# A mixture-of-experts layer: where the shared expert's last product stands between wide and single expert jobs

## The chip, the core and the metric

The kernel runs on one core of a Trainium2 chip. The metric is device time in microseconds (us) of one whole execution; three executions of the kernel before gave 2105.7, 2106.51 and 2108.94 us, with a median of 2106.51 us. PE is the matrix engine, DVE the vector engine, ACT the scalar engine, POOL the general-purpose engine, and SP the engine that here only issues transfers. All of them run their own instruction streams and meet through semaphores.

## The reference, cut to what matters

Two graph layers run over 625 nodes of 1024 features. Each adds a graph branch, an attention branch and a feed-forward branch. The change lies in the last piece, the feed-forward branch of the second layer: a small attention, a router that sends every node to two of eight experts, and a shared expert that sees every node.

```python
logits = xf @ Wr.T + expert_bias
rw = jax.nn.softmax(logits, axis=-1)
topw, topi = jax.lax.top_k(rw, TOP_K)          # TOP_K = 2 of 8 experts
topw = jax.nn.softmax(topw, axis=-1)
...
shared = _swiglu(xf, sW1, sW2, sW3)             # silu(x @ W1.T) * (x @ W3.T) @ W2.T
...
eo = jnp.einsum('etf,edf->etd', h, eW2)         # the same form for every expert
specialist = jnp.einsum('te,etd->td', combine, eo)
moe_out = (shared + specialist).reshape(B, S, d)
return X + moe_out
```

The shared expert's last product is the multiplication by `sW2`, a matrix of 1024 by 1024 in float32 (4 MB).

## The kernel before, in words

Nodes stand in NT = 5 tiles of P = 125 rows. Everything is float32, and a product of two float32 tiles shows in the profile as two matrix instructions.

**What comes before.** The shared expert's first two products make `hT`, all nodes' hidden values turned so that the features lie on the partitions. They are made by `eighth(0)` and `eighth(1)`, each with seven smaller products (a Strassen scheme, named p1 to p7 by their role). The second of them runs p1, p2, p6, p7, p4, p5, p3. The products p1, p2 and p4 read the tile `tT` (the normalised nodes, turned); p5, p6, p7 and p3 read sums made from it. p4 is the last to read `tT`. Up to this point the order of every engine, SP too, is the order in which the program is written (`hand`, a manual schedule, closed on L2192). After it the Tile scheduler orders instructions inside each basic block, unless another manual schedule is opened.

**The routed experts.** The router's counts are made on the chip. Each expert's nodes are cut into blocks of up to 128 rows, and two jobs exist for them. A wide job (`wide_job`, L2242) takes up to 192 rows of an expert at once, with the weights as the stationary operand. A single job (`block`, L2214) takes one block of 128 rows. Each job loads three 4 MB matrices of its expert in twelve transfers of 1 MB on SP (`Half`, L126, six buffers of tag `w` for the first two matrices and four of tag `mid` for the third), fetches its rows with an indirect transfer on POOL (`take`, L2201), turns them on PE (`turned`, L2211), multiplies, and writes its result to the DRAM table `y_d`.

**Branches.** How many jobs there are is known only on the chip. So `wides` (L2284), `odd` (L2290) and `fours` (L2296) are nested `If`s; every engine loads the count into a register (`count_of`, L2280) and branches for itself. An engine that leaves the branch without taking it first waits for its own earlier work and then raises its semaphores by what the skipped jobs would have raised, so that later waits still count right. On this input the profile shows two wide jobs, no odd block and eight blocks in two groups of four.

**The shared expert's last product.** After the wide jobs, SP is told to load `sW2` in eight transfers of 512 KB: `k` 0 to 4 into a buffer of tag `big`, 5 to 7 into the buffer of tag `CT` (L2308). `big` has two buffers; at that time one holds `hT`, and the other `three`, the single tile with the wide jobs' three operands (rows turned, hidden values, result). `sw2` takes the buffer of `three`.

**The end.** After the last block, PE, DVE and POOL follow a hand-written order. `fetch(t)` (L2325) gathers a node tile's two expert results from `y_d` with two indirect transfers into buffers of tags `xg` and `yb` (two of each); `shared(t)` (L2331) multiplies one node tile by `sW2`, in two groups of eight products into one PSUM bank each (`ps1`, two buffers), and DVE adds each half to `x` (L2336); `routed(t)` (L2340) adds the two gathered results on DVE; SP writes the tile out (L223). The order is `fetch(0)`, `fetch(1)`, then for each tile but the last `shared`, `routed`, `fetch(t + 2)`, and for the last one `routed` before `shared`.

Of the kernel before, what the change touches and what calls it, by code (L numbers as in the profile page):

```python
# [8 lines left out]
FP = mybir.dt.float32  # L9
# [5 lines left out]
ALU = mybir.AluOpType  # L15
# [6 lines left out]
P = 125  # L22
NP = 626
# [6 lines left out]
D = 1024  # L30
KC = D // 128
NE = 8
# [3 lines left out]
WIDE = 192  # L36
# [19 lines left out]
def attempt(ctx: ExitStack, tc: tile.TileContext, w: dict, out: bass.AP, shifted: bool):  # L56

    nc = tc.nc
# [6 lines left out]
    def ps1(name):  # L65
        pool, n = psums[-1]
        return pool.tile([128, 512], FP, tag="ps1", name=name, bufs=n)

    def ps2(name):
        return psums[-1][0].tile([128, 2, 512], FP, tag="ps2", name=name, bufs=3)  # L70
# [65 lines left out]
    def group(dst, pairs):  # L136

        for i, (lhsT, rhs) in enumerate(pairs):
            made = nc.tensor.matmul(dst, lhsT=lhsT, rhs=rhs, start=(i == 0), stop=(i == len(pairs) - 1))  # L139
        latest["pe"] = made.ins.name  # L140
# [60 lines left out]
    def nodes(t):  # L201
        return slice(t * P, (t + 1) * P)
# [24 lines left out]
    gpool = graph.enter_context(tc.tile_pool(name="graph", bufs=1))  # L227
    CTr = gpool.tile([P, NT, NP], FP if shifted else FR, tag="CT", name="CT")
    CT = CTr if shifted else CTr.bitcast(FP)
# [176 lines left out]
    with ExitStack() as st0:  # L406
# [493 lines left out]
        x = xpool.tile([P, NT, D], FP, name="x")  # L900
# [1084 lines left out]
    nc.gpsimd.dma_start(out=eb_t, in_=w["expert_bias"].to_broadcast([P, NE]))  # L1985
    lg = pool.tile([P, NT, NE], FP, name="lg")

    lgT = pool.tile([NE, NP], FP, name="lgT")

    def logits():  # L1990
        hold["plT"] = ps2("plgT")
# [194 lines left out]
    then.fourth()  # L2186
    p7_()
    p4_()
    p5_()
    p3_()  # L2190
    do.flush()
# [7 lines left out]
    def take(b, n=128):  # L2199
        xg = pool.tile([128, D], FP, tag="xg", name="xg", bufs=2)[:n]  # L2200
        nc.gpsimd.indirect_dma_start(out=xg, out_offset=None, in_=rows_d[:, :],  # L2201
                                     in_offset=bass.IndirectOffsetOnAxis(ap=slots[0:n, b:b + 1], axis=0))
        return xg

    def turned(name, xg, dst):
        n = xg.shape[0]
        for h in range(2):
            p = ps1(name).rearrange("p (c n) -> p c n", c=4)[:, :, 0:n]
            for c in range(4):
                k = 4 * h + c  # L2210
                nc.tensor.transpose(p[:, c, :], xg[:, k * 128:(k + 1) * 128], ident[:n, :n])  # L2211
            by_gain(dst[:, 4 * h:4 * h + 4, :], p, 1, h, n)

    def block(b):  # L2214

        W1, W3, W2 = expert(b)
        xg = take(b)
        xgT = pool.tile([128, KC, 128], FP, tag="xgT", name="xgT", bufs=2)
        turned("pxg", xg, xgT)
        hb = pool.tile([128, KC, 128], FP, tag="hb", name="hb", bufs=2)  # L2220
        for c in range(2):
            w1, w3 = Half(wpool, W1, c), Half(wpool, W3, c)
            pu = ps2("pu")
            group(pu[:, 0, :], [(xgT[:, k, :], w1(k)) for k in range(KC)])
            group(pu[:, 1, :], [(xgT[:, k, :], w3(k)) for k in range(KC)])
            su = pool.tile([128, 512], FP, tag="su", name="su", bufs=2, padded_shape=[128, 2 * HN])
            nc.scalar.activation(su, pu[:, 0, :], AF.Sigmoid)  # L2227
            nc.vector.tensor_tensor(su, pu[:, 0, :], su, op=ALU.mult)  # L2228
            nc.vector.tensor_tensor(su, pu[:, 1, :], su, op=ALU.mult)
            p = ps1("phb").rearrange("p (c n) -> p c n", c=4)  # L2230
            for a in range(4):
                nc.tensor.transpose(p[:, a, :], su[:, a * 128:(a + 1) * 128], ident)
            copy(hb[:, 4 * c:4 * c + 4, :], p)
        yb = pool.tile([128, D], FP, tag="yb", name="yb", bufs=2)
        py = ps2("pyb")
        for c in range(2):
            w2 = Half(midp, W2, c, tag="mid", padded=[128, 4, 645])
            group(py[:, c, :], [(hb[:, k, :], w2(k)) for k in range(KC)])
            copy(yb[:, c * 512:(c + 1) * 512], py[:, c, :])
        nc.scalar.dma_start(out=y_d[b * 128:(b + 1) * 128, :], in_=yb)  # L2240

    def wide_job(i):  # L2242
        W1, W3, W2 = expert(NS + i)
        b = NS + 2 * i
        xgT, hb, yT = (three[:, j] for j in range(3))
        turned("pxg", take(b), xgT[:, :, 0:128])
        turned("pxh", take(b + 1, WIDE - 128), xgT[:, :, 128:WIDE])
        for c in range(2):
            w1, w3 = Half(wpool, W1, c), Half(wpool, W3, c)
            for m in (0, 2):  # L2250
                pu = ps2("puw")
                for j, wt in enumerate((w1, w3)):
                    for a in range(2):
                        group(pu[:, j, a * WIDE:(a + 1) * WIDE], [(wt(k, (m + a) * 128, 128), xgT[:, k, :])
                                                                  for k in range(KC)])
                su = pool.tile([128, 2 * WIDE], FP, tag="su", name="su", bufs=2, padded_shape=[128, 2 * HN])
                nc.scalar.activation(su, pu[:, 0, 0:2 * WIDE], AF.Sigmoid)
                nc.vector.tensor_tensor(su, pu[:, 0, 0:2 * WIDE], su, op=ALU.mult)
                nc.vector.tensor_tensor(hb[:, 4 * c + m:4 * c + m + 2, :],
                                        pu[:, 1, 0:2 * WIDE].rearrange("p (a n) -> p a n", a=2),  # L2260
                                        su.rearrange("p (a n) -> p a n", a=2), op=ALU.mult)
        for c in range(2):
            w2 = Half(midp, W2, c, tag="mid", padded=[128, 4, 645])
            for m in (0, 2):
                p = ps1("pyT")[:, 0:2 * WIDE].rearrange("p (a n) -> p a n", a=2)
                for a in range(2):
                    group(p[:, a, :], [(w2(k, (m + a) * 128, 128), hb[:, k, :]) for k in range(KC)])
                copy(yT[:, 4 * c + m:4 * c + m + 2, :], p)
        for part, lo, n in ((b, 0, 128), (b + 1, 128, WIDE - 128)):
            yb = pool.tile([128, D], FP, tag="yb", name="yb", bufs=2)[:n]  # L2270
            py = ps2("pyw")
            for k in range(KC):
                nc.tensor.transpose(py[:n, k // 4, (k % 4) * 128:(k % 4 + 1) * 128], yT[:, k, lo:lo + n], ident)
            for c in range(2):
                copy(yb[:, c * 512:(c + 1) * 512], py[:n, c, :])
            nc.scalar.dma_start(out=y_d[part * 128:part * 128 + n, :], in_=yb)
# [22 lines left out]
            if 4 * i + 8 < NS:  # L2299
                fours(i + 1)  # L2300

    three = big.tile([128, 3, KC, WIDE], FP, tag="big", name="three")
    n_wide = count_of(1, NW)
    wides(0)
    sw2 = [big.tile([128, 5, D], FP, tag="big", name="sw2"), gpool.tile([128, 3, D], FP, tag="CT", name="sw2b")]
    sw2_v = w["sW2"].rearrange("(k p) n -> p k n", p=128)
    for k in range(KC):
        nc.sync.dma_start(out=sw2[k // 5][:, k % 5, :], in_=sw2_v[:, k, :])  # L2308
    n_odd = count_of(0, 3)
    odd(0)  # L2310
    n_fours = count_of(2, 4)
# [7 lines left out]
    with tc.manual_schedule(engines={mybir.EngineType.PE, mybir.EngineType.DVE, mybir.EngineType.Pool}):  # L2319
        def fetch(t):  # L2320

            pair = []
            for i, (tag, n) in enumerate((("xg", 2), ("yb", 2))):
                yg = pool.tile([128, D], FP, tag=tag, name="yg", bufs=n)
                nc.gpsimd.indirect_dma_start(out=yg, out_offset=None, in_=y_d[:, :],  # L2325
                                             in_offset=bass.IndirectOffsetOnAxis(ap=place[:, i, t:t + 1], axis=0))
                pair.append(yg)
            return pair

        def shared(t):  # L2330
            for c in range(2):  # L2331
                pp = ps1("py")
                group(pp[:P], [(hT[:, k, nodes(t)], sw2[k // 5][:, k % 5, c * 512:(c + 1) * 512])
                               for k in range(KC)])
                xc = x[:, t, c * 512:(c + 1) * 512]
                nc.vector.tensor_tensor(xc, pp[:P], xc, op=ALU.add)  # L2336

        def routed(t, pair):
            for yg, weight in zip(pair, (p1, e2)):
                nc.vector.scalar_tensor_tensor(x[:, t, :], yg[:P], weight[:, t:t + 1], x[:, t, :],  # L2340
                                               op0=ALU.mult, op1=ALU.add)

        pairs = [fetch(0), fetch(1)]
        for t in range(NT):
            if t < NT - 1:
                shared(t)
                routed(t, pairs[t])
            else:
                routed(t, pairs[t])
                shared(t)  # L2350
            if t + 2 < NT:
                pairs.append(fetch(t + 2))
            rows_dma(nc.sync, out[nodes(t), :], x[:, t, :])
# [87 lines left out]
```

## Time and profile before

| what | us |
|---|---|
| median of three runs | 2106.51 |
| the profiled execution's own time | 2111.3 |
| its span, first to last instruction | 2109.5 |
| two wide jobs (PE) | 1508.1 to 1648.0 |
| from there to the first product of the single jobs | 1648.0 to 1667.25 |
| eight single jobs (PE) | 1667.25 to 2018.1 |
| last product of the shared expert (PE) | 2019.5 to 2101.5 |

The times in the table's lower rows are counted from the span's start. In the profile, `L139 PE MATMUL py<-sw,hT` means: line 139 of the kernel (the helper `group`), matrix engine, output tile `py`, made from `sw` and `hT`. "PE" with a q behind it is the engine's sequencer, which branches, waits on semaphores and hands instructions to the engine. What stands in square brackets in a timeline is how long the engine was idle before the row, and what ended it.

### The profile page before, as it was taken

To read this page: it belongs to the slowest core of one execution; us is meant where nothing else is said; L and a number is where in the kernel's file an instruction comes from. 1 tells how busy PE (TensorE), PEld (TensorE's weight loads), DVE (VectorE), ACT (ScalarE), POOL (GpSimd) and SP (SyncE) were. 2 spreads that over 40 slices of the span, in tenths; PEclk is the share of its full clock that TensorE was granted. 3 is DMA by queue.
4 is the path that set the end of the run, shared out by engine and by line. 5 is a ranking of instruction groups with operands and counts; after the bars stand their busy time and mean duration, and the time that the engine had idled before them with its cause. 6 is when DMAs were issued, how large, how long until landed. Compare 5 with 4: busy or idle time off the path is not lost. (4 is left out here: it accounts for less than half of the span.)

```text
span 2109.5 us, 18497 instructions
## 1 busy us (share of the span) xinstructions
PE 2009.6 (95%) x7366; PEld 1264.2 (60%) x7366; DVE 855.2 (41%) x1344; ACT 201.8 (10%) x369; POOL 309.2 (15%) x324
## 2 busy tenths in 40 slices
PE   7999999499999999999999999999999699999988
PEld 6665575255445787787467776466799444444433
DVE  5786387477431772353341324265210011111112
ACT  2110110011211100000000111111000000000000
POOL 1777757300000000000000001100000000000011
PEclk9999999799999999999999999999999899999989
DMA  6632263360122112222251435221363698788732
GB/s 215 224 111 83 85 212 111 77 189 1 40 90 80 40 41 80 80 80 80 80 179 50 140 120 200 71 79 58 112 253 122 224 372 326 279 303 319 265 120 81
DMA packets 155398, 299.20 MB, mean 142 GB/s; under 512 B 12316, under 2 KB 50083, under 8 KB 155287
## 3 DMA queue, kind: packets, MB, share of 16 engines
q1 hardware_dynamic: 131228, 234.72, 32.0%
q0 software_dynamic: 19200, 53.34, 7.8%
q10 hardware_dynamic: 4858, 9.70, 1.5%
q8 instruction: 66, 1.08, 0.2%
q14 instruction: 46, 0.37, 0.1%
HBM read 260.19 MB, written 37.52 MB: 141 GB/s over the span
## 5 line engine op out<-in xcount | busy, mean ns | idle before, releaser
L139 PE MATMUL pu<-w,xgT 128*128 128x512 f32 x512 | 224.2, 596 | 3.2 <-DMA w<-in_eW_dram 2.6
L139 PEld LDWEIGHTS pu<-w,xgT 128*128 128x128 f32 x512 | 96.7, 191 | 119.5 <-issue 118.8
L139 PE MATMUL pk<-w,xnT 128*125 128x512 f32 x320 | 143.5, 602 | 2.2 <-ACT xnT L1108 2.2
L139 PE MATMUL pv<-w,xnT 128*125 128x512 f32 x320 | 140.8, 593 | 0.9 <-DVE x L990 0.9
L139 PE MATMUL pq<-xnT,w 128*128 128x313 f32 x512 | 137.5, 427 | 0.8 <-DVE v L336 0.8
L139 PEld LDWEIGHTS pq<-xnT,w 128*128 128x128 f32 x512 | 96.9, 190 | 39.2 <-DVE v L336 1.6
L139 PE MATMUL pyb<-w,hb 128*128 128x512 f32 x256 | 116.2, 598 | 1.7 <-ACT yb L107 1.5
L139 PEld LDWEIGHTS pk<-w,xnT 128*125 128x125 f32 x320 | 60.2, 191 | 75.8 <-issue 72.9
L139 PEld LDWEIGHTS pv<-w,xnT 128*125 128x125 f32 x320 | 59.4, 188 | 73.5 <-issue 71.3
L809 PE MATMUL px<-w,oT 128*125 128x512 f32 x160 | 72.4, 611 | 29.3 <-DMA table<-es,at 28.0
L2228 DVE TENSOR_TENSOR su<-pu,su 128x512 f32<-128x512 f32 x16 | 11.1, 691 | 213.7 <-ACT su L2227 213.7
L684 POOL DMA_INDIRECT table<-es,at x79 | 85.7, 1085 | 59.2 <-issue 27.3
L139 PE MATMUL puw<-three,w 128*128 128x192 f32 x512 | 87.1, 335 | 0.0
L139 PEld LDWEIGHTS puw<-three,w 128*128 128x128 f32 x512 | 86.5, 196 | 0.1
L2201 POOL DMA_INDIRECT xg<-rows_d,slots x12 | 11.6, 967 | 497.9 <-PE pxg L2211 288.9
L664 POOL DMA_INDIRECT ga<-xl_d,si x79 | 79.5, 1007 | 30.2 <-issue 21.1
L139 PEld LDWEIGHTS pyb<-w,hb 128*128 128x128 f32 x256 | 46.6, 189 | 60.7 <-issue 49.9
L664 POOL DMA_INDIRECT gb<-xr_d,di x79 | 78.4, 992 | 24.1 <-issue 21.6
L809 PEld LDWEIGHTS px<-w,oT 128*125 128x125 f32 x160 | 30.6, 194 | 69.0 <-issue 36.7
L139 PE MATMUL ph<-S,wq 128*128 128x313 f32 x256 | 70.4, 435 | 0.0
L139 PE MATMUL pX<-w,aT 128*125 128x512 f32 x160 | 69.3, 592 | 0.0
L166 DVE TENSOR_TENSOR wq<-wq,wq 128x2048 f32<-128x2048 f32 x28 | 63.9, 2283 | 12.8 <-PE pw L139 7.5
(442 smaller groups left out, 2877.8 us busy)
## 6 DMA issues: line engine op xcount, KB each, us to landing
w<-in_eW_dram SPq DMA_DIRECT2D x120, 1024.0 KB
y_d<-zero POOLq DMA_DIRECT2D x9, 2048.0 KB, 10.6
w<-in_L_Wk_dram SPq DMA_DIRECT2D x8, 1024.0 KB
w<-in_L_Wv_dram SPq DMA_DIRECT2D x8, 1024.0 KB
w<-in_L_Wq_dram SPq DMA_DIRECT2D x8, 1024.0 KB
w<-in_L_Wo_dram SPq DMA_DIRECT2D x8, 1024.0 KB
wq<-in_W_self_dram SPq DMA_DIRECT2D x8, 1024.0 KB
wq<-in_W_neigh_dram SPq DMA_DIRECT2D x8, 1024.0 KB
```

Of the source, the lines that this page charges most:

```text
L139: made = nc.tensor.matmul(dst, lhsT=lhsT, rhs=rhs, start=(i == 0), stop=(i == len(pairs) - 1))
L166: nc.vector.tensor_tensor(self.tiles[dst], self.tiles[a], self.tiles[b], op=op)
L664: got = nc.gpsimd.indirect_dma_start(out=ab[g][side][0:p, j, :], out_offset=None, in_=src[:, :], in_offset=bass.IndirectOffsetOnAxis(ap=ix ...
L684: put = nc.gpsimd.indirect_dma_start(out=table[:, :], out_offset=bass.IndirectOffsetOnAxis(ap=at[0:p, lo + j:lo + j + 1], axis=0), in_=es[ ...
L809: made = nc.tensor.matmul(hold["px", t][:P, c, :], lhsT=oT[:, k, nodes(t)], rhs=wo[c](k), start=(k == 0), stop=(k == KC - 1 and keep is no ...
L2201: nc.gpsimd.indirect_dma_start(out=xg, out_offset=None, in_=rows_d[:, :], in_offset=bass.IndirectOffsetOnAxis(ap=slots[0:n, b:b + 1], axis=0))
L2228: nc.vector.tensor_tensor(su, pu[:, 0, :], su, op=ALU.mult)
```

## The change

1. `sW2` is loaded earlier: its eight transfers stand on SP behind p4 of `eighth(1)`, inside the manual schedule, in the order `k` = 7 down to 0. `sw2` now takes the buffer of `tT`.
2. `three` goes. The wide jobs' three operands, and the single jobs' `xgT` and `hb`, come from one ring of three buffers of tag `xt` (`operand`).
3. A wide job's rows are turned into PSUM tiles of two banks (`ps2`) instead of two of one bank.
4. `shared(0)` and `shared(1)` stand between the wide jobs and `odd(0)`, in a manual schedule for PE and DVE. `shared(2)`, `shared(3)` and `shared(4)` stay at the end.
5. `lgT`, the router's logits, takes a buffer of tag `yb` instead of its own.

```diff
-    lgT = pool.tile([NE, NP], FP, name="lgT")
+    lgT = pool.tile([128, D], FP, tag="yb", name="lgT", bufs=2)[:NE, :NP]
...
     p7_()
     p4_()
+    sw2 = [big.tile([128, 5, D], FP, tag="big", name="sw2"), gpool.tile([128, 3, D], FP, tag="CT", name="sw2b")]
+    sw2_v = w["sW2"].rearrange("(k p) n -> p k n", p=128)
+    for k in reversed(range(KC)):
+        nc.sync.dma_start(out=sw2[k // 5][:, k % 5, :], in_=sw2_v[:, k, :])
     p5_()
     p3_()
     do.flush()
...
+    def operand(name, n=128):
+        return pool.tile([128, KC, n], FP, tag="xt", name=name, bufs=3, padded_shape=[128, KC, WIDE])
+
-    def turned(name, xg, dst):
+    def turned(name, xg, dst, two=False):
         n = xg.shape[0]
+        both = [v for v in ps2(name).rearrange("p h (c n) -> h p c n", c=4)] if two else None
         for h in range(2):
-            p = ps1(name).rearrange("p (c n) -> p c n", c=4)[:, :, 0:n]
+            p = (both[h] if two else ps1(name).rearrange("p (c n) -> p c n", c=4))[:, :, 0:n]
...
-        xgT = pool.tile([128, KC, 128], FP, tag="xgT", name="xgT", bufs=2)
+        xgT = operand("xgT")
         turned("pxg", xg, xgT)
-        hb = pool.tile([128, KC, 128], FP, tag="hb", name="hb", bufs=2)
+        hb = operand("hb")
...
-        xgT, hb, yT = (three[:, j] for j in range(3))
-        turned("pxg", take(b), xgT[:, :, 0:128])
-        turned("pxh", take(b + 1, WIDE - 128), xgT[:, :, 128:WIDE])
+        xgT = operand("xwT", WIDE)
+        turned("pxg", take(b), xgT[:, :, 0:128], True)
+        turned("pxh", take(b + 1, WIDE - 128), xgT[:, :, 128:WIDE], True)
+        hb = operand("hw", WIDE)
...
+        yT = operand("yT", WIDE)
...
-    three = big.tile([128, 3, KC, WIDE], FP, tag="big", name="three")
     n_wide = count_of(1, NW)
     wides(0)
-    sw2 = [...]                                  (the two tiles and the eight transfers above)
+    with tc.manual_schedule(engines={mybir.EngineType.PE, mybir.EngineType.DVE}):
+        shared(0)
+        shared(1)
     n_odd = count_of(0, 3)
     odd(0)
...
         for t in range(NT):
             if t < NT - 1:
-                shared(t)
+                if t > 1:
+                    shared(t)
                 routed(t, pairs[t])
             else:
                 routed(t, pairs[t])
```

`shared` itself is unchanged; it only moves out of the last manual schedule, ahead of its first call.

More of the change, by code (lines that the diff above doesn't have):

```diff
@@ L2300, in fours, with shared @@
                 fours(i + 1)
-    three = big.tile([128, 3, KC, WIDE], FP, tag="big", name="three")
+    def shared(t):
+        for c in range(2):
+            pp = ps1("py")
+            group(pp[:P], [(hT[:, k, nodes(t)], sw2[k // 5][:, k % 5, c * 512:(c + 1) * 512])
+                           for k in range(KC)])
+            xc = x[:, t, c * 512:(c + 1) * 512]
+            nc.vector.tensor_tensor(xc, pp[:P], xc, op=ALU.add)
     n_wide = count_of(1, NW)
     wides(0)
[L2305 to L2308, printed above, removed]
+    with tc.manual_schedule(engines={mybir.EngineType.PE, mybir.EngineType.DVE}):
+        shared(0)
+        shared(1)
     n_odd = count_of(0, 3)
@@ L2328, in fetch @@
             return pair
[L2330 to L2336, printed above, removed]
         def routed(t, pair):
```

## The prediction

> **What bounds the kernel now.** I first read the page's chain of work that ended last, then PE's timeline at the end, because the chain has only PE and one transfer in it.
>
> ```profile
> PE 3%; DMA 0%; SPq 0%; DVE 0%; issue 0%
> PE py L139 3%; DMA sw<-in_sW_dram 0%; SPq L2308 0%; DVE x L2336 0%; SPq L2296 0%
> ```
> The end hangs on `py`, the product by `sW2`, and on the landing of `sw`. PE's timeline shows how:
>
> ```profile
> 2019.50 1.12 PE L139 MATMUL py<-sw,hT 128*125 128x512 f32 x2 [1.41 <-ACTq L2296]
> 2025.80 3.56 PE L139 MATMUL py<-sw,hT 128*125 128x512 f32 x4 [5.18 <-DMA sw<-in_sW_dram]
> 2030.38 1.12 PE L139 MATMUL py<-sw,hT 128*125 128x512 f32 x2 [1.01 <-DMA sw<-in_sW_dram]
> 2032.92 2.07 PE L139 MATMUL py<-sw,hT 128*125 128x512 f32 x2 [1.43 <-DMA sw<-in_sW_dram]
> ...
> 2094.45 4.45 PE L139 MATMUL py<-sw,hT 128*125 128x512 f32 x10
> 2098.74 2.74 PE L139 MATMUL py<-sw2b,hT 128*125 128x512 f32 x6
> ```
> Groups of 16 instructions follow each other every 6.87 us (2046.38, 2053.25, ... in the same timeline). Ten groups are 68.7 us, but PE takes from 2019.50 to 2101.49, 82.0 us. So 13.3 us are lost: four of the eight pieces of `sW2` are issued only from 2022.08, behind the last branch, and while PE waits for them its granted clock falls to half.
>
> The second place is the passage from wide to single jobs. The timelines of PE and POOL, and the line of the `odd` branch:
>
> ```profile
> 1645.93 2.02 PE L2273 MATMUL pyw<-ident,three 128*128 128x128 f32 x16
> 1662.69 1.94 PE L2211 MATMUL pxg<-ident,xg 128*128 128x128 f32 x8 [14.74 <-DMA xg<-rows_d,slots]
> 1667.25 5.27 PE L139 MATMUL pu<-w,xgT 128*128 128x512 f32 x8 [2.62 <-DMA w<-in_eW_dram]
> ```
> ```profile
> 1656.71 0.94 POOL L2201 DMA_INDIRECT xg<-rows_d,slots  x1 [143.11 <-SPq L2290]
> ```
> ```profile
> L2290 PEldq COMPARE_BRANCH  x1: 4479/4479/4479, 1651.8 to 1651.8; - x1
> ...
> L2290 PEldq EVENT_SEMAPHORE  x1: 51/51/51, 1656.4 to 1656.4; - x1
> ```
> PE is idle for 14.7 us and again for 2.6 us, 17.4 us in which moved work might lie. But read the times: PE's branch past the odd blocks takes 4.48 us, PE raises its semaphore for the skipped blocks at 1656.43 (start plus 51 ns), and POOL's gather starts at 1656.71. The profile names SP as releaser; SP's increments on that line run on to 1656.9, so that label is not safe. The gather overwrites a buffer whose last readers in program order are PE's turns in the skipped odd blocks, so I take PE's increment as what it waits for. SP's weight loads overwrite `w` buffers with the same readers; the first is issued at 1658.66.
>
> **The end, part by part.** The stall of 13.3 us goes if `sW2` is there. Three tiles are 6 × 6.87 = 41.2 us. DVE's new order puts `routed(0)` and `routed(1)` ahead of any `shared` add, and PE has only two PSUM buffers for `py`. The four gathers are issued at 2022.4 to 2026.1 as before; in the trace a gather pair takes about 8 us from issue to landing (2048.86 to 2057 and 2051.03 to 2058, the landings as DMA semaphore times), and without 2 MB of `sW2` beside them I put the fourth at about 2034. DVE then ends `routed(1)` (2 × 1.3 us) at 2035 and frees the first PSUM buffer at 2035.9, where PE wanted it at 2019.5 + 13.7 = 2033.2: 2.7 us lost (0 if the gathers land 3 us sooner, 5 if 2 us later), and about 1 us (0 to 1.7) for a half-clock window after that pause. Afterwards the gathers of tiles 2 to 4 come 8 us behind each `routed`, at about 2039, 2043 and 2050, while PE's last group begins at about 2056: they stay hidden. So 44.9 us instead of 82.0: **−37.1**. The last add and the output transfers behind it (8.0 us to 2109.5) stay.
>
> **The middle.** Added: 4 groups × 6.87 = 27.5 us of PE, from about 1650.7 (PE leaves L2284 at 1650.5). What of it is hidden depends on three things.
>
> (a) The branch. The Trainium skill, "Runtime: NRT & Kernel Launch", section "Instruction fetch mechanics", says that a taken branch to a target outside the fetched pages stalls the engine until the page arrives. The 4.48 us row agrees in kind, and by the rule alone register load (1.2 us) and branch would follow the moved product exposed. But another row of the same kind:
>
> ```profile
> L2296 PEldq COMPARE_BRANCH  x1: 3435/3435/3435, 2011.0 to 2011.0; - x1
> ```
> stands in a stretch where PE's products run without a break from 2010.95 to 2018.1 (the last 16 of the last job). PE's sequencer is a whole group ahead, so the stall lies under queued products. At 1651.8 nothing was queued. After the change a group of 16 is: I take load and branch, 5.8 us from 1650.6 to 1656.4, as hidden; exposed, they cost up to 5.8 more.
>
> (b) The loads behind the branch. If gather and weights wait for PE's increment, they don't start under the moved product, but 0.1 to 0.3 us after it. Before, 10.8 us passed from the increment to the first `pu`: gather 6.2, turning and the DVE scaling to about 8.2, then the weights, which SP issued 2.2 us after the increment behind a 512 KB piece of `sW2`. That piece is gone and SP stands ready, so the gather's path decides: 8.8 us (8.2 to 10.8).
>
> (c) The clock. "TensorE: Matmul & The Clock Gate", Part 1, has the clock fall after an idle window of some 3.4 us; PE is idle 2.7 us here, so by the rule the moved product could start warm. The trace's rows by stretch say otherwise, with the granted clock in the third place from the right:
>
> ```profile
> 1648.50:1649.50 1.00, 0.00 (x0) 0.00 (x0) 0.72 (x2) 0.07 (x1) 0.00 (x0) 1.00 0.10 41
> 1650.50:1651.50 1.00, 0.00 (x0) 0.00 (x0) 0.00 (x0) 0.00 (x0) 0.00 (x0) 0.50 1.01 274
> ```
> The clock is halved by 1650.5. A half-clock stretch of about 3 us costs 1.4 us (0 by the rule, 1.7 at most for one window of that length).
>
> Sum: 1650.7 + 27.5 + 1.4 + 0.2 (last product to increment) = 1679.8, plus 8.8 = 1688.6 for the first `pu`, against 1667.25: **+21.3**.
>
> **Loads of `sW2` ahead.** Eight issues of about 0.42 us each (the L2308 rows) are added to SP ahead of the wide job's twelve. The first three go at once (`CT` is long free). The fourth waits for p4, the last reader of `tT`, which PE ends at 1491.2 (it starts p5 there). Behind it on SP stand the register load, the branch and wide job 1's weights, of which the trace has four issued at 1449.22 to 1491.41. They now go at about 1496.5 (1491.4 + 5 × 0.42 + 3 for load and branch, as 1428.9 to 1431.7 before). At 381 GB/s (the busiest stretch, 1662 to 1672) the 2.6 MB of `sW2` are in by about 1500, the first two pieces by 1506, the next two by 1511. PE wants the first two at 1512.4 and the others 5.4 us later: **0**, covered by p5 and p3, with 6 us of slack; each us beyond it is a us lost. If the buffer came free only with p3, at 1508.3, it would cost about 10.
>
> **The rest.** `ps2` for the turns ends a wait of 2.2 and 1.2 us of PE on DVE, but the four scalings on DVE set the start of the product either way: 0 (−0.3 to +0.3). The ring of three: a block's `xgT` takes the buffer of the `hb` two jobs back, its `hb` that of the previous `xgT`, both read out by then: 0 (up to +3 if the scheduler orders the blocks otherwise). `lgT` shares with `X` of tile 3, read out 25 us before: 0.
>
> **Sum.** −37.1 + 21.3 = −15.8. The profiled span 2109.5 becomes 2093.7. That execution took 2111.3 with what lies around the span, 4.8 above the median; I take the difference off the median: 2106.5 − 15.8 = **2090.7**.
>
> **Rivals.**
> 1. The loads do run under the moved product (the label "SPq L2290" is right and PE's increment isn't needed). Then `pu` starts at 1679.8 plus about 2.2 for turning: +14.7 instead of 21.3, giving 2084. For it: the label. Against: 0.3 us between PE's increment and the gather, after SP had branched at 1653.8.
> 2. The branch isn't hidden, or the gathers hold DVE and PSUM at the end for longer: 3 to 8 us more, 2097. For it: 4.48 us were exposed once, and the end's gathers have little slack. Against: the row at 2011.0.
> 3. Slower: SP stands at the fourth piece of `sW2` for longer than p4, and wide job 1 waits for its weights. Place: SP between the shared expert's loads and the wide jobs. Beyond a release at about 1499 each us costs one; it decides from about 1515, where the loss equals the 15.8. Released at 1525 it gives 2117. Against: nothing behind p4 reads `tT`.
> 4. The moved product gives back all it saves: both the odd branch and the loads exposed (+27) and the end bound by its gathers (−27): 2106, no change.
>
> **How the numbers follow.** Forecast 0.60; rival 1 0.12; rival 2 0.18; rival 3 0.07, of which 0.01 still ends faster; rival 4 0.03. That is faster 0.91, same 0.03, slower 0.06, where 0.2% (4.2 us) is about what a measurement of this kernel can tell from no change. The forecast's own terms (stall at the end 0 to 6.7, loads 8.2 to 10.8, clock 0 to 1.7) make 2086 to 2095. The range takes in rivals 1 and 2 with a us for each: 2083 to 2100.
>
> **What would show it.** `py` in four groups from about 1650.7, the first MATMULs at half clock; PE's branch on the `odd` line starting before the last of them ends; POOL's gather within 0.5 us of PE's increment; `pu` near 1688; at the end six groups without a wait for `sw`, and a pause of PE on DVE ahead of the third. Wrong would make it: a wait for `w` ahead of `puw` in wide job 1; a gather far ahead of PE's increment; a PE stall at the end above 7 us.

## The result and the profile after

The changed kernel takes 2090.05 us in the median (2087.92 to 2094.16), against 2106.16 us for the kernel before in the same comparison: a ratio of 0.9921, with a 95% interval of 0.9908 to 0.9934. That is 16.1 us less by the medians; the forecast was 15.8. A ratio below 1 means faster than the kernel before, here and in what follows.

The page's chain of work that ended last, with its shares by engine and by line:

```profile
PE 1%; DMA 0%; DVE 0%; issue 0%; POOL 0%; POOLq 0%
PE py L139 1%; DMA yg<-y_d,place 0%; DVE x L2348 0%; DVE x L2318 0%; POOL yg L2341 0%; POOLq L2341 0%
```

`sw` is gone from it. The chain now runs back from PE through DVE to the landing of the gathered results `yg`: the pause ahead of the third group at the end, which PE's timeline shows as a wait for DVE (in square brackets the idle time before the row, and its releaser):

```profile
2036.20 4.56 PE L139 MATMUL py<-sw,hT 128*125 128x512 f32 x10 [1.41 <-ACTq L2306]
...
2047.46 2.74 PE L139 MATMUL py<-sw2b,hT 128*125 128x512 f32 x6
2051.60 4.56 PE L139 MATMUL py<-sw,hT 128*125 128x512 f32 x10 [1.39 <-DVE x L2318]
...
2076.59 2.74 PE L139 MATMUL py<-sw2b,hT 128*125 128x512 f32 x6
```

Six groups take 43.1 us, where ten took 82.0. In the passage from wide to single jobs, PE and POOL did this:

```profile
1640.19 2.02 PE L2283 MATMUL pyw<-ident,yT 128*128 128x128 f32 x16
1645.49 6.21 PE L139 MATMUL py<-sw,hT 128*125 128x512 f32 x10 [3.29 <-PEq L2294]
...
1672.14 2.74 PE L139 MATMUL py<-sw2b,hT 128*125 128x512 f32 x6
1682.79 1.94 PE L2219 MATMUL pxg<-ident,xg 128*128 128x128 f32 x8 [7.91 <-DMA xg<-rows_d,slots]
1684.73 15.69 PE L139 MATMUL pu<-w,xgT 128*128 128x512 f32 x34
```
```profile
1675.24 0.95 POOL L2205 DMA_INDIRECT xg<-rows_d,slots  x1 [164.79 <-PEq L2300]
```

and the line of the `odd` branch, L2300 by now, for PE's sequencer (`COMPARE_BRANCH` is the branch, `EVENT_SEMAPHORE` the increment):

```profile
L2300 PEldq COMPARE_BRANCH  x1: 3942/3942/3942, 1667.4 to 1667.4; - x1
L2300 PEldq EVENT_SEMAPHORE  x1: 51/51/51, 1674.9 to 1674.9; - x1
```

and, on the same line, for SP:

```profile
L2300 SPq EVENT_SEMAPHORE  x9: 17/17/17, 1648.2 to 1650.4; - x9
```

The branch takes 3.9 us from 1667.4, while PE's products run without a break up to 1674.9. PE raises its semaphore at 1674.9, and the gather starts at 1675.24, in this trace with PE named as releaser; SP's own increments had ended at 1650.4. So the moved product covers the branch, and nothing of the gather.

Single executions of one kernel differ by up to 8 us on the faster chips and by up to 27 us on a slower one. The part ahead of the wide jobs, in which the change adds only the issues of `sW2` on SP, ended at 1504.1 us in this profile and at 1508.1 in that of before (and at 1532 to 1541 on other chips). So the stages below are compared from the first turn of rows in wide job 1 on. Each is read from PE's timeline.

| stage (us) | before | changed | forecast difference | measured |
|---|---|---|---|---|
| wide jobs, first turn to the start of the last turns of results (`pyw`) | 137.8 | 136.1 | 0 | −1.7 |
| from there to the first `pu` | 21.3 | 44.5 | +21.3 | +23.2 |
| single jobs, first `pu` to the start of the last `pyb` instruction | 350.3 | 349.5 | 0 | −0.8 |
| to the first `py` at the end | 2.0 | 2.0 | 0 | 0.0 |
| `py` at the end | 82.0 | 43.1 | −37.1 | −38.9 |
| to the end of the span | 8.1 | 7.8 | 0 | −0.3 |
| sum | 601.4 | 583.0 | −15.8 | −18.4 |

The 18.4 us of these two profiles lie inside the interval of the timed ratio (13.9 to 19.4 us of 2106).

### The profile page after: what moved, and what is told of

Read it like the earlier page. It is cut to its first block, busy times and chain, and to the rows that moved or that the text cites. A ratio compares the mean times of both kernels' runs of the same rounds, so it can differ in the third digit from the quotient of the medians.

```text
span 2087.1 us, 18497 instructions
## 1 busy us (share of the span) xinstructions
PE 2003.5 (96%) x7366; PEld 1261.8 (60%) x7366; DVE 855.4 (41%) x1344; ACT 201.8 (10%) x369; POOL 308.7 (15%) x324
## 5 line engine op out<-in xcount | busy, mean ns | idle before, releaser
L139 PE MATMUL puw<-xwT,w 128*128 128x192 f32 x512 | 85.4, 331 | 0.0
L139 PEld LDWEIGHTS puw<-xwT,w 128*128 128x128 f32 x512 | 84.8, 193 | 0.1
```

## The experiments

The theory (A): the gain is the stall of 13 us at the end; the move covers only the branch past the odd blocks, since gather and weights wait for the increment that PE makes behind that branch. The rivals: the idle passage hides the moved product (B); SP or POOL, and not PE, sets the start of the gather; the turns into two-bank tiles or the release of `sW2`'s buffer matter. The times of each run are compared with those of the kernel before on the same chip, its stages with the two profiles above.

**sW2 ahead alone.**

```diff
     wides(0)
-    with tc.manual_schedule(engines={mybir.EngineType.PE, mybir.EngineType.DVE}):
-        shared(0)
-        shared(1)
...
-                if t > 1:
-                    shared(t)
+                shared(t)
```

> Undoes the move alone: sW2 is loaded early as in the changed kernel, but all five tiles of the shared expert's last product stand at the end. Theory A (the gain is the stall at the end; the move pays for itself only by the branch that it hides): the end is ten groups without a wait for sw, 68.7 us instead of 82.0, and the passage from wide to single jobs is 1.5 to 2.5 us shorter than before, since the 512 KB piece no longer lies ahead of the weights; together about 15 us under the kernel before, 2091 us, within 2 us of the changed kernel. Rival B (the moved product lies in the idle passage and most of the gain is the move): 13 us of stall gone at most, and the changed kernel should be 8 us or more below this one, so this one would be at 2098 or more. The passage tells it too: A has the first pu 19 to 20 us after the last turn of the wide jobs begins.

Measured: 2093.92 us against 2109.33, a ratio of 0.9933 (0.9916 to 0.9950); 585.8 us from the first turn on, 15.6 under the kernel before. PE's timeline of this kernel in the passage and at the start of the end:

```profile
1640.92 2.01 PE L2283 MATMUL pyw<-ident,yT 128*128 128x128 f32 x16
1656.95 1.94 PE L2219 MATMUL pxg<-ident,xg 128*128 128x128 f32 x8 [14.02 <-DMA xg<-rows_d,slots]
1660.36 21.11 PE L139 MATMUL pu<-w,xgT 128*128 128x512 f32 x42 [1.47 <-DMA w<-in_eW_dram]
...
2013.82 4.56 PE L139 MATMUL py<-sw,hT 128*125 128x512 f32 x10 [1.41 <-ACTq L2306]
2018.21 2.74 PE L139 MATMUL py<-sw2b,hT 128*125 128x512 f32 x6
2020.79 4.46 PE L139 MATMUL py<-sw,hT 128*125 128x512 f32 x10
```

The ten groups at the end follow each other at 6.87 us and take 68.9 us; the passage takes 19.4. Both are theory A's numbers. The early load is worth 13.1 us at the end and 1.9 in the passage, and the move of two tiles the 2.8 us that remain to the changed kernel's 583.0. Of these, 2.0 lie in the single jobs: without the move, PE's clock is still half for the first 5.7 us of them, in the changed kernel for the first 1.7. Where the stall at the end came from, the issues of `sW2` in the kernel before show:

```profile
L2308 SPq DMA_DIRECT2D sw<-in_sW_dram x5: 354/418/432, 1657.1 to 2023.4; - x5
L2308 SPq DMA_DIRECT2D sw2b<-in_sW_dram x3: 347/427/430, 1108.0 to 1108.9; - x3
```

All eight are written behind the wide jobs, yet three went at 1108, one at 1657 and four behind the last branch. Rival B, which put most of the gain into the move, falls by the trace; the timed medians alone, some 2 to 4 us apart, would not decide it.

**Both tiles behind the odd branch.**

```diff
     wides(0)
-    with tc.manual_schedule(engines={mybir.EngineType.PE, mybir.EngineType.DVE}):
-        shared(0)
-        shared(1)
     n_odd = count_of(0, 3)
     odd(0)
+    with tc.manual_schedule(engines={mybir.EngineType.PE, mybir.EngineType.DVE}):
+        shared(0)
+        shared(1)
```

> Moves the two tiles from ahead of the odd branch to behind it. Theory A: PE's branch past the odd blocks (4 to 4.5 us) and the register load stand exposed again, but PE raises its semaphore for the skipped blocks ahead of the product, so gather and weights run under it. From the end of the wide jobs' branch to the first pu about 37.3 us instead of 39.4, with the single jobs starting on a warm clock (0.9 less): about 3 us under the changed kernel, 2087 us. The gather is issued within 0.5 us of PE's increment, some 27 us ahead of the end of the product. Rival (SP's or POOL's own branch gates the gather): it is issued at the same time against the wide jobs' end as in the kernel before whatever PE does, and the sum would be 4 to 6 us above the changed kernel, 2095, since only the branch is lost.

Measured: 2088.4 us, ratio 0.9908 (0.9885 to 0.9931); 579.3 us from the first turn on, 3.6 under the changed kernel. Its PE and POOL timelines, and the increments on the branch line:

```profile
1640.66 2.02 PE L2283 MATMUL pyw<-ident,yT 128*128 128x128 f32 x16
1651.19 6.97 PE L139 MATMUL py<-sw,hT 128*125 128x512 f32 x10 [8.51 <-PEq L2300]
...
1682.12 0.66 PE L2219 MATMUL pxg<-ident,xg 128*128 128x128 f32 x4 [0.35 <-DVE x L2318]
1682.71 9.71 PE L139 MATMUL pu<-w,xgT 128*128 128x512 f32 x22
```
```profile
1651.14 0.95 POOL L2205 DMA_INDIRECT xg<-rows_d,slots  x1 [140.21 <-SPq L2300]
```
```profile
L2300 SPq EVENT_SEMAPHORE  x9: 17/17/17, 1648.7 to 1650.9; - x9
...
L2300 PEldq EVENT_SEMAPHORE  x1: 51/51/51, 1650.8 to 1650.8; - x1
```

Now PE waits 8.5 us at the branch, which lies open, and the gather goes at 1651.14, right behind PE's increment at 1650.8 and 30 us ahead of the end of the product. The label says SP here, whose own increments run on to 1650.9, so by this trace alone either could be it. The changed kernel's trace tells them apart: there the gather follows PE's increment within 0.3 us as well, and SP had made its own increments 24 us before. With one tile on each side (next) PE's increment is at 1665.0 and the gather at 1665.28, 10 us behind SP's last.

**One tile on each side.**

```diff
-        shared(0)
-        shared(1)
+        shared(0)
     n_odd = count_of(0, 3)
     odd(0)
+    with tc.manual_schedule(engines={mybir.EngineType.PE, mybir.EngineType.DVE}):
+        shared(1)
```

> One tile ahead of the odd branch and one behind it. Theory A: the first tile's last group hides branch and register load (5.8 us), the second tile's 13.7 us hide gather and weights (7 to 8 us); from the end of the wide jobs' branch to the first pu about 31.8 us instead of 39.4, no pause of PE above 1.5 us in between, single jobs warm from the start: 8 to 8.5 us under the changed kernel, 2082 us. Rival: if the pauses were set by something else than these two (the weights' transfers at full rate, or the order of SP), splitting brings the smaller of the two gains at most, 2087 or more.

Measured: 574.9 us from the first turn on, 8.0 under the changed kernel, as theory A has it. The timed ratio, 0.9908 (0.9887 to 0.9930, median 2088.15 instead of the expected 2082), shows only part of that: it stands for 14.8 to 23.8 us under the kernel before, where the two profiles differ by 26.5, and it doesn't tell this version from the one with both tiles behind the branch. What the stages gain is thus shown by the trace, and not yet by the times. PE's timeline:

```profile
1644.48 2.02 PE L2283 MATMUL pyw<-ident,yT 128*128 128x128 f32 x16
1649.25 6.22 PE L139 MATMUL py<-sw,hT 128*125 128x512 f32 x10 [2.75 <-ACTq L2294]
...
1665.85 4.53 PE L139 MATMUL py<-sw,hT 128*125 128x512 f32 x10 [0.93 <-DVEq L2300]
...
1680.60 0.66 PE L2219 MATMUL pxg<-ident,xg 128*128 128x128 f32 x4 [0.35 <-DVE x L2318]
1681.19 11.00 PE L139 MATMUL pu<-w,xgT 128*128 128x512 f32 x25
```

The branch cost lies under the first tile and the transfers under the second: of the idle time, 0.9 and 0.35 us are left behind the first product. The passage takes 36.7 us instead of 44.5. The first product runs at half clock here too (6.22 us for ten instead of 4.46), after a pause of PE of only 2.75 us.

**Turns in single banks.**

```diff
-        turned("pxg", take(b), xgT[:, :, 0:128], True)
-        turned("pxh", take(b + 1, WIDE - 128), xgT[:, :, 128:WIDE], True)
+        turned("pxg", take(b), xgT[:, :, 0:128])
+        turned("pxh", take(b + 1, WIDE - 128), xgT[:, :, 128:WIDE])
```

> Undoes the turns into two-bank tiles alone: the wide jobs' rows are turned into single-bank tiles again. Prediction's step: nothing, 2090 us, because DVE's four scalings set the start of the product either way. The changed kernel's wide jobs took 1.7 us less than before, and its trace has one half-clock window in them where before had two. Theory P (phase of the window by chance): no change beyond 1.7 us either way from run to run. Rival T (the turns' pause of PE on DVE, 1.2 us in job 2, brings the half clock): the second window comes back with this kernel at the start of wide job 2, and the time rises by about 1.7 us, to 2092.

Measured: 2092.35 us, ratio 0.9918 (0.9902 to 0.9935). The wide jobs take 136.1 us as in the changed kernel, with one half-clock stretch in them, and the whole from the first turn on 583.2. PE waits 1.1 us for DVE in job 2, and no second stretch comes with it: rival T falls. This part of the change is worth nothing, as forecast.

**A later release of sW2's place (all of it behind p3).**

```diff
-    for k in reversed(range(KC)):
-        nc.sync.dma_start(out=sw2[k // 5][:, k % 5, :], in_=sw2_v[:, k, :])
     p5_()
     p3_()
+    for k in reversed(range(KC)):
+        behind(nc.sync.dma_start(out=sw2[k // 5][:, k % 5, :], in_=sw2_v[:, k, :]), latest["pe"])
```

> Measures rival 3's price: all eight transfers of sW2 wait for the last product of p3 instead of p4 and of nothing, about 17 us later on SP (1504 instead of 1487 in the changed kernel's trace), everything else as in the changed kernel. Prediction's step: 6 us of slack, then one us for each us, so that a release with p3 costs about 10: SP issues the eight pieces in 3.5 us and then wide job 1's weights at about 1509; at 340 to 380 GB/s the 4 MB of sW2 take 11 to 12 us, the first weights land at about 1519 and the next at 1522 instead of before 1508.4. The first puw begins 10 to 13 us later against the first turn of rows (which stays where it was), and the run ends that much later: about 2102 us. Rival: SP's place costs nothing because PE is covered (by the turns and the half-clock window): under 3 us.

Measured, on another, slower chip: 2144.96 us against 2137.76 for the kernel before there, a ratio of 1.0028 (1.0007 to 1.0048), so slightly slower than the kernel before. But it doesn't measure what it was made for. Though all eight pieces are written ahead of wide job 1, only two were issued there, and six behind the wide jobs, from 1686.9; why is not shown. PE's timeline has both bills:

```profile
1542.80 4.18 PE L139 MATMUL puw<-xwT,w 128*128 128x192 f32 x12 [5.59 <-DMA w<-in_eW_dram]
1549.40 10.80 PE L139 MATMUL puw<-xwT,w 128*128 128x192 f32 x65 [2.42 <-DMA w<-in_eW_dram]
...
1697.58 6.24 PE L139 MATMUL py<-sw,hT 128*125 128x512 f32 x10 [16.30 <-SPq L2300]
```

The weights of wide job 1, issued at 1535.1, came 8 us late in two waits, and the moved product stood until its `sW2` had landed (the trace has the last landing at 1697.4, though the row names SP), 18.3 us behind the start of the last turns instead of 5.1 (in the changed kernel's second profile, below). So rival 3's mechanism exists. The sign was turned by both bills together; the forecast was off because the pieces stood elsewhere.

**The same with the order kept.** Pieces 4 to 0 wait for p5, 8.5 us later than p4:

```diff
+    p5_()
     for k in reversed(range(KC)):
-        nc.sync.dma_start(out=sw2[k // 5][:, k % 5, :], in_=sw2_v[:, k, :])
-    p5_()
+        put = nc.sync.dma_start(out=sw2[k // 5][:, k % 5, :], in_=sw2_v[:, k, :])
+        if k == 4:
+            behind(put, latest["pe"])
     p3_()
```

> The price of a later release of sW2's place, with a release that keeps all eight pieces ahead of wide job 1 on SP: pieces 4 to 0 wait for the end of p5 instead of p4, 8.5 us later; pieces 7 to 5 go as in the changed kernel. Prediction's step: 6 us of slack, each us beyond it lost, so 2 to 3 us. By the changed kernel's own landings (weights of the first product in at 1499.0 and 1501.7, wanted at 1508.4 and 1509.7; of the second at 1504.4 and 1507.3, wanted at 1513.8 and 1515): a shift of 8.5 costs 0.5 to 1 at the first and up to 1 more at the second. From the first turn of rows to the first puw 4.8 instead of 4.2 us, wide jobs 137 to 138 us instead of 136.1. Rival: nothing, under 0.3, because SP's issue isn't what the weights wait for.

Measured, in one execution: the wide jobs take 140.6 us, 4.5 more than in the changed kernel. Its waits:

```profile
1547.92 6.41 PE L139 MATMUL puw<-xwT,w 128*128 128x192 f32 x38 [0.17 <-DMA w<-in_eW_dram]
1556.51 3.90 PE L139 MATMUL puw<-xwT,w 128*128 128x192 f32 x12 [2.17 <-DMA w<-in_eW_dram]
```

The waits for weights are 2.3 us, which is what a slack of 6 us would leave of a shift of 8.5. But that agreement is luck. The long wait is for the fourth 1 MB piece: it landed 15.2 us behind the first turn instead of 3.1, so 12 us later and not 8.5, and had had a slack of 10.8 us. The gathers of the second wide job's rows, issued at 1545.5 and 1546.7, now ran beside it; that they made the difference is not shown. The other 2 us were not forecast: this trace has two half-clock stretches in the wide jobs, one right behind the wait at 1556.5 and one in the second job, and the changed kernel's trace has one. The first `puw` began on time (4.2 us behind the first turn).

**The pause at the end.** First with product and add in turn, on top of the split:

```diff
+        both = ps2("py") if t > 1 else None
         for c in range(2):
-            pp = ps1("py")
+            pp = both[:, c, :] if t > 1 else ps1("py")
```

> The split of the run before last (one tile ahead of the odd branch, one behind it) with one more edit: at the end the product's two halves go into a tile of two PSUM banks, of which there are three, instead of two single banks. If the pause of PE ahead of the third group at the end (1.4 to 1.7 us over the pace of 0.43 in the changed kernel and in the split) is a wait for a PSUM buffer that DVE holds behind the gathered results, it goes, and the end falls from 43.1 to 43.5 us to 41.4: 2081 us or less in the median if the split is worth its 8 us. Rival: the pause is PE waiting for something else (its own next weights, a semaphore of the branch), and the end stays at 43.

Measured: 2121.88 us on the slower chip, ratio 0.9931 (0.9903 to 0.9959). The end takes 54.6 us, 11 more than the split's:

```profile
2060.92 2.74 PE L139 MATMUL py<-sw2b,hT 128*125 128x512 f32 x6
2071.84 7.12 PE L139 MATMUL py<-sw,hT 128*125 128x512 f32 x10 [8.18 <-DVE x L2319]
```

Neither case expected this. PE now waits between the two halves of one tile for DVE's add of the first half: written in turn, a product into the second half of a tile waits for the read of the first. So the edit made a new wait, worse than the one that it was to end. With both products ahead of both adds:

```diff
+        both = ps2("py") if t > 1 else None
+        parts = [both[:, c, :] if t > 1 else ps1("py") for c in range(2)]
-        for c in range(2):
-            pp = ps1("py")
+        for c, pp in enumerate(parts):
             group(pp[:P], [...])
+        for c, pp in enumerate(parts):
             xc = x[:, t, c * 512:(c + 1) * 512]
             nc.vector.tensor_tensor(xc, pp[:P], xc, op=ALU.add)
```

> The split again (one tile ahead of the odd branch, one behind it) and the two-bank tile at the end, but with both halves' products written in the program ahead of DVE's two adds. In the run with product, add, product, add PE stood 8.8 us between the two halves of one tile, behind DVE's add of the first half, which stands behind the gathered results: the tile was waited for as a whole. Written so, PE fills a tile and goes on to the next of three; no tile is waited for at the end, which falls to about 41.4 us, and from the first turn of rows to the end of the span to about 573 us (574.9 for the split alone, 583.0 for the changed kernel). The median should be 8 to 10 us under the changed kernel's. Rival: the pause comes back ahead of the third group as 1.4 us or more, so that it isn't a wait for PSUM.

Measured: 2107.9 us against 2138.01 for the kernel before on the same chip, a ratio of 0.9869 (0.9835 to 0.9903), and 573.0 us from the first turn on.

```profile
2055.33 4.56 PE L139 MATMUL py<-sw,hT 128*125 128x512 f32 x10 [0.90 <-DVEq L2306]
2059.73 2.74 PE L139 MATMUL py<-sw2b,hT 128*125 128x512 f32 x6
2062.30 4.46 PE L139 MATMUL py<-sw,hT 128*125 128x512 f32 x10
2066.59 2.74 PE L139 MATMUL py<-sw2b,hT 128*125 128x512 f32 x6
2069.17 4.46 PE L139 MATMUL py<-sw,hT 128*125 128x512 f32 x10
```

The third group starts without a pause, and the end takes 41.5 us. This version is faster than both kernels by its stages: 28.4 us under the kernel before and 10 under the changed one. That its 573.0 us meet the forecast is luck in part: against the split the wide jobs took 1.7 us less, without a half-clock stretch, and the passage 1.6 more, with one of 6.8 us instead of 3.4. Its timed interval lies below the changed kernel's first one (0.9908 to 0.9934), but overlaps the one taken on another chip (0.9883 to 0.9948, below), so that the times alone make the second difference likely rather than sure.

**The changed kernel again**, beside the first version with two-bank tiles:

> The changed kernel again, on the same chip as the version above, so that both stand against the same runs of the kernel before. Theory A: 16 us under the kernel before in the median; the part of the trace from the first turn of rows to the end of the span about 583 us (601.4 before), the part ahead of it 1504 to 1509 us whichever of the kernels runs, since nothing in it is changed that PE waits for.

Measured: 2118.96 us, ratio 0.9915 (0.9883 to 0.9948); 582.1 us from the first turn on, with all stages within 0.5 us of the first profile. What makes this chip slower lies ahead of the wide jobs, which begin at 1532.1 and not, as expected, at 1504 to 1509.

## Why the prediction was right

- **The sum, −15.8.** The stages add up to −18.4, the medians to −16.1. The mechanism of both main terms was right. That the median agrees within 0.3 us is luck in part: the misses of middle and end, +1.9 and −1.8, cancel, 2.5 us in the wide and single jobs were not forecast, and the executions of this kernel spread over 6 us.
- **The end, −37.1.** Right; −38.9. The six groups are 41.2 us as counted. The wait for a PSUM buffer was put at 2.7 us and is 1.6 (2.0 from one product to the next instead of 0.43), because the gathers landed sooner (DVE ends `routed(1)` 14.7 us behind the first product at the end, where 15.5 was put); the half-clock stretch behind it, put at 1 us, didn't come. That it is a wait for PSUM is shown by the version with both products ahead of both adds, where it goes with a third tile.
- **The middle, +21.3.** Right in its three parts, 1.9 us too small in sum. (a) The branch is hidden: it starts at 1667.4, 7.5 us ahead of the end of the queued products. The Trainium skill's rule on taken branches ("Runtime: NRT & Kernel Launch", "Instruction fetch mechanics") agrees with the sequencer's 3.9 us row, but no run here shows that this time is the fetch of a page; it becomes time of the kernel only where nothing is queued, as the version with both tiles behind the branch shows (8.5 us of idle PE). (b) The transfers are not hidden. From the increment to the first `pu` it takes 9.8 us, not 8.8: the gather lands 7.4 us after its issue, not the 5.9 of before. The weights' issues now start 0.2 us ahead of it; before, they started 2 us behind it, with one piece of `sW2` between. In the version with `sW2` ahead alone they start 0.7 us behind it, and the gather lands after 5.1 us. The traces agree with this as the reason, but no run changed this order alone. (c) The clock is half at the start of the moved product:

```profile
1646.00:1648.00 2.00, 2.00 (x3) 0.67 (x2) 0.00 (x0) 0.00 (x0) 0.00 (x0) 0.50 0.08 23
```

  It costs 1.75 us (the first ten products 6.21 us instead of 4.46), where 1.4 was put and 1.7 was the most. Here the granted clock had been followed rather than the Trainium skill's idle window of 3.4 us ("TensorE: Matmul & The Clock Gate", Part 1), and rightly: PE had been idle for 3.3 us, and in the split for only 2.75, with the clock half all the same. The start itself came 0.5 us later than put.
- **Loads of sW2 ahead, 0.** Right: the first `puw` starts 4.2 us behind the first turn, as before. The slack, put at 6 us, was 7.2 at the tightest (a piece landed at 1501.6 and was waited for at 1508.8). The price past the slack was put at one for one; the one execution that bears on it lost 4.5 us where 2 to 3 were expected.
- **The rest, 0.** Right for the turns in the number, but the two-bank tiles did not end PE's wait on DVE. It only moved, to between the two halves of a tile:

```profile
1504.65 0.46 PE L2219 MATMUL pxh<-ident,xg 64*128 64x64 f32 x4
1507.37 0.66 PE L2219 MATMUL pxg<-ident,xg 128*128 128x128 f32 x4 [2.26 <-DVE xwT L1513]
```

  It is 2.3 us in the first job and 1.1 in the second, as before, and the same kind of wait as in the first version with product and add in turn. The single jobs took 0.8 us less, since the half clock reaches 1.7 us into them instead of 3.3; the prediction had counted no half clock there. The wide jobs took 1.7 less because one half-clock stretch was missing. Whether that is the change's is open: the same wide-job code had one stretch in six profiles, two in the two with `sW2` late and none in the one with both products ahead of both adds; single banks didn't bring the second one back, and the kernel before was profiled once. The ring of three buffers and the place of `lgT` were not undone by themselves.
- **Rivals.** 1 fell by the gather's time. 2 fell: hidden branch, shorter pause. 3 fell for this change, and its mechanism was seen in the versions with `sW2` late. 4 fell.

## What to carry to other kernels

A stretch of idle time isn't room for moved work until it is known what starts the work behind it: here the transfers waited for an increment that PE makes only behind the moved product, so the passage grew by 23.2 us for 27.5 us of moved product, and 17 us of idle PE took in little more than 4. Put one piece ahead of the branch to cover the branch, and one behind it to cover the transfers: with one tile on each side the passage was 7.8 us shorter. And a transfer that a scheduler is free to place should be looked up in the issuing queue: of the 15.6 us that the early load gained by itself, 13.1 were a stall behind four 512 KB pieces that had been issued behind the last branch.

## What the runs showed of the hardware

The branch past the odd blocks takes PE's sequencer 3.3 to 4.5 us in these traces, and the other engines' branch instructions on that line under 0.1 us. From 1400 us on, every half-clock stretch that lies whole inside a trace lasts 3.4 us or a multiple of it (6.8 us at the moved product of the version with both products ahead of both adds, 20.5 in the passage of the kernel before). One of 3.4 us under full work costs 1.7 us: the first products of a wide job (`puw`) take 43.55 us with one and 41.87 without. The same wide-job code had two, one or none of them, so a difference of 2 to 3 us between two single profiles can be this alone. And in both places where a two-bank tile was filled and read in turn, PE waited between its halves for DVE's read of the first: 8.2 us at the end, 2.3 in the first turns.
